# Second layer of a four-layer network: how recurrence work is dealt out over expert tiles and returning rows

## The chip, the cores and the metric

The kernel runs on one core of one Trainium2 chip, as one launch. The metric is the device time of an execution in microseconds, the median over several runs. The engines are named as in the profile: PE is TensorE, with PEld its weight loads; DVE is VectorE; ACT is ScalarE; POOL is GpSimd; SP is SyncE, which issues most DMAs.

## What is computed

Four layers follow each other; each normalises x, runs a token mixer (giving s) and a gate network (giving g), and adds s times silu(g) to x. There are 4096 tokens of 128 features: 8 sequences ("batches" in the code) of 512. The change lies in layer 1 (the second one), whose mixer is a recurrence over time and whose gate network is a mixture of experts. Cut to what matters:

```
# mixer, per sequence; r = sigmoid(mixed(xn) @ Wr); k, v = mixed(xn) @ Wk, Wv
def step(carry, kv):
    num, den, mx = carry
    max_out = maximum(mx, k + tf)
    e1, e2 = exp(mx - max_out), exp(k + tf - max_out)
    out = (e1 * num + e2 * v) / (e1 * den + e2)
    max_st = maximum(mx + td, k)
    e1s, e2s = exp(mx + td - max_st), exp(k - max_st)
    return (e1s * num + e2s * v, e1s * den + e2s, max_st), out
s = (r * out) @ Wo
# gate network: 8 routed experts, 2 per token, and 2 shared ones
g = sum_over_chosen(weight * ffn_e(xn)) + sum_over_shared(ffn_e(xn))
x = x + s * silu(g)
```

## The kernel before

Activations stay in SBUF with features on the partitions, 512 tokens (one sequence) to a block. In layer 1 `l1_layer` makes the programs of several engines go together by Python generators. All its instructions are issued through wrappers that keep the order of the code on each engine (`in_order`, so the profile gives line 82 for all of them; they are told apart by their tiles). Each engine executes its own instructions in order and waits for others by semaphores.

**The recurrence.** `attend(b)` (line 507) does one sequence in 13 parts, ended by `yield`: k; v (two products each on TensorE, copied by ScalarE); a scan for the running maximum `mx`; e1s and e2s; `mo` and e1; e2 and one Exp over all four (ScalarE, 128x2048); `ev` and the scan `num`; the scan `den` and `up`; two operations on `v` and `up`; two on `dn`; the reciprocal of `dn` (128x512); two products on `up`; and the output product `ps_o` on TensorE with its copy into s. Below, "parts" are these, and the digit before a name is the sequence. `attention(batches)` runs sequences one after the other.

**The tiles.** `experts.tiles` (line 777) works on 72 tiles of 128 gathered token rows, two in each of 36 steps, plus two steps to drain. Step t has: gathers on POOL five steps ahead (`xr`), register loads of the next expert numbers on TensorE (`which`, which may be moved earlier, as they are not held in order), the first products `ps_ab` into the two PSUM banks of `p_a`, Silu (`sa`, ScalarE) and the product `hh` (VectorE), transposes `tp_h` of the step before, second products `ps_y` of the step before that, their copy `yy` (VectorE) and its write into `yrows` by SP, and transposes `tp_g` of rows for t+2. At the end of each step parts are drawn from `between`:

```
                while done < n_between * (t + 1) // (T + 2):
                    next(between, None)
                    done += 1
```

Before, 60 parts (12 x 5) are drawn so, of the 65 of sequences 0 to 4; `for _ in between: pass` then issues the remaining five by themselves.

**The returning rows.** `experts.rows_back` (line 877) does, for each sequence b, the shared experts in four pieces (`first`: products `pa`, `pb`, Silu `a`, product `h` on VectorE; `second`: product into `acc`), then `back`: eight products that add the gathered expert rows `yr` to `acc`, and `gated`: Silu `sg`, `pr`, x. The gathers of `yr` read `yrows`, 8 per sequence, two sequences ahead (16 buffers). `first` is issued one piece ahead of `second`. After each `second` two parts are drawn, as long as b is under 5; these are sequences 5 to 7. `gated(b)` reads s of sequence b.

After this layer come the normalisation of layer 2 and the other layers, which the change does not touch.

## Time and profile before

| | |
|---|---|
| median of 5 runs | 2903.58 us (2897.37 to 2912.3) |
| profiled execution | 2910.07 us, its span 2908.4 us |
| busy: PE, DVE, ACT, POOL | 2604.9, 2195.1, 1858.4, 1552.4 us |
| first `ps_ab` of the tiles, last `ps_y` | 555.38, 739.86 us |
| first and last `acc<-ident,yr` (`back`) | 775.98, 898.69 us |
| busy in 549 to 738 us: PE, DVE, ACT | 153.74, 105.19, 85.36 us |
| busy in 738 to 757 us: PE, DVE, ACT | 4.05, 16.12, 4.75 us |
| busy in 776 to 901 us: PE, DVE, ACT | 102.51, 68.84, 36.93 us |

A row of the timeline gives start, duration, engine, line, operation, tile written and tiles read, number of instructions merged, and in brackets the idle time of that engine before it and what ended that. A group of instructions gives busy time and, behind the comma, the mean duration of one in ns; behind the bar stands the idle time of the engine just before them. A waits row gives who waited for whom: total us, times, longest.

### The profile page before, as it was taken

The page shows a single profiled execution, that of the slowest core. Times are in us where ns is not written, and L with a number is a line of the kernel's source. Part 1 is how long each engine was busy: PE and PEld are TensorE (multiplying, and loading weights), DVE is VectorE, ACT ScalarE, POOL GpSimd, SP SyncE. Part 2 cuts the span into 40 slices and gives each one's busy share as a digit, 9 for nine tenths or more (in the row PEclk, how much of TensorE's full clock was granted, in tenths as well). Part 3 has the DMA queues.
Part 4 walks back from the last instruction along what each step waited for, and adds up shares of the span by engine and source line. Part 5 has one row for each costly group of instructions (what it writes and reads, how often), then busy time and mean ns, then how long its engine had stood idle before and what let it go on. Part 6 is the DMA issues. An engine that isn't in the chain of part 4 may idle for free. (4 is left out here: it accounts for less than half of the span.)

```text
span 2908.4 us, 48757 instructions
## 1 busy us (share of the span) xinstructions
PE 2604.9 (90%) x18636; PEld 1821.2 (63%) x18636; DVE 2195.1 (75%) x2907; ACT 1858.4 (64%) x3601; POOL 1552.4 (53%) x1262
## 2 busy tenths in 40 slices
PE   7999898778778788886899999999999999999897
PEld 4656676455335555555677777777777777767675
DVE  4666554566563655554999999999999999999565
ACT  2566443245331554544698988989898888888634
POOL 2444322442342232225667778787777778787323
PEclk7899797999898888886999999999999999999979
DMA  1000002012100000002222222222122222222100
GB/s 47 2 2 2 1 1 85 24 51 50 31 28 19 2 2 2 2 1 98 60 54 59 61 61 60 61 60 55 50 64 58 61 60 61 60 52 51 25 1 30
DMA packets 56311, 112.73 MB, mean 39 GB/s; under 512 B 10768, under 2 KB 28752, under 8 KB 55440
## 3 DMA queue, kind: packets, MB, share of 16 engines
q1 hardware_dynamic: 51584, 99.40, 13.0%
q0 software_dynamic: 4352, 8.92, 1.3%
q8 instruction: 148, 2.42, 0.4%
q10 hardware_dynamic: 144, 1.31, 0.1%
q14 instruction: 83, 0.68, 0.1%
HBM read 30.43 MB, written 12.06 MB: 15 GB/s over the span
## 5 line engine op out<-in xcount | busy, mean ns | idle before, releaser
L82 POOL TENSOR_TENSOR ek<-E,kn 128x512 f32<-128x512 f32 (+3 forms) x512 | 427.7, 869 | 62.6 <-ACT kn L82 61.6
L82 POOL TENSOR_TENSOR r<-r,rs 128x1024 f32<-128x1024 f32 x128 | 317.6, 2481 | 258.4 <-DMA rs<-r 200.0
L82 POOL TENSOR_TENSOR e<-e,mx 128x1024 f32<-128x1024 f32 x112 | 212.8, 1900 | 375.2 <-DVE mx L82 287.2
L82 ACT ACTIVATE y<-y,mx 128x256 f32<-128x256 f32 (+3 forms) x512 | 287.1, 562 | 102.8 <-DVE mx L82 102.8
L82 PE MATMUL sc<-r 128*128 128x512 f32 (+3 forms) x1024 | 308.0, 444 | 24.9 <-POOL r L82 19.0
L82 PEld LDWEIGHTS ps_av<-u,at 128*128 128x128 f32 x2560 | 301.8, 192 | 41.0 <-ACT at L82 31.5
L82 PE MATMUL ps_av<-u,at 128*128 128x128 f32 x2560 | 314.7, 278 | 6.2 <-ACT at L82 6.2
L82 PEld LDWEIGHTS sc<-r 128*128 128x128 f32 x1024 | 166.2, 192 | 177.3 <-issue 70.4
L82 DVE SCALAR_TENSOR_TENSOR y<-sc,qn,V 128x512 f32<-128x512 f32 (+3 forms) x512 | 246.0, 543 | 2.3
L82 ACT ACT_TABLE_LOAD x181 | 232.2, 1283 | 4.3 <-PE pa L82 1.2
L82 DVE TENSOR_REDUCE mx<-y 128x2 f32<-128x768 f32 (+3 forms) x256 | 207.7, 812 | 1.7
L82 DVE SCALAR_TENSOR_TENSOR y<-y,coef,G 128x2560 f32<-128x2560 f32 x64 | 198.4, 3100 | 4.7 <-ACT y L82 2.3
L82 DVE SCALAR_TENSOR_TENSOR sc<-sc,ek 128x1280 f32<-128x1280 f32 x128 | 191.3, 1495 | 11.8 <-PE sc L82 6.2
L82 PE MATMUL tp<-ident,y 128*128 128x128 f32 x1280 | 197.9, 277 | 1.3 <-ACT y L82 0.8
L82 ACT COPY at<-tp 128x512 f32<-128x512 f32 (+1 forms) x384 | 188.5, 513 | 6.5 <-PE tp L82 6.4
L82 DVE TENSOR_TENSOR sc<-sc,E 128x1280 f32<-128x1280 f32 x128 | 191.1, 1493 | 0.0
L82 PEld LDWEIGHTS tp<-ident,y 128*128 128x128 f32 x1280 | 153.2, 146 | 41.7 <-issue 18.3
L82 POOL TENSOR_TENSOR s<-s,o 128x512 f32<-128x512 f32 x120 | 157.7, 1314 | 29.6 <-ACT o L82 29.6
L82 PEld LDWEIGHTS ps_u<-wvo,xn 128*128 128x128 f32 x1024 | 128.2, 191 | 70.0 <-DVE qn L82 57.0
L82 DVE TENSOR_TENSOR r<-sn,ps_kq 128x1024 f32<-128x1024 f32 x128 | 155.0, 1211 | 7.6 <-ACT sq L82 4.1
L82 ACT ACTIVATE y<-y 128x2560 f32<-128x2560 f32 x64 | 149.7, 2340 | 15.1 <-DVE y L82 7.7
L82 ACT COPY pt<-tp 128x512 f32<-128x512 f32 x224 | 121.0, 585 | 58.8 <-PE tp L82 58.6
(396 smaller groups left out, 5847.1 us busy)
## 6 DMA issues: line engine op xcount, KB each, us to landing
rs<-r SPq DMA_DIRECT2D x256, 256.0 KB
yrows<-yy SPq DMA_DIRECT2D x36, 128.0 KB
ct<-trig SPq DMA_DIRECT2D x16, 256.0 KB
m_w<-m_w SPq DMA_DIRECT2D x1, 2560.0 KB
x<-x SPq DMA_DIRECT2D x8, 256.0 KB
xrows<-row SPq DMA_DIRECT2D x8, 256.0 KB
sn<-trig SPq DMA_DIRECT2D x32, 64.0 KB
sn<-trig SPq DMA_DIRECT2D x16, 128.0 KB
```

The lines of the kernel that those rows point to most:

```text
L82: ins = op(*args, **kwargs)
```

## The change

The reciprocal of `dn` becomes four of 128x128, each a part of its own. An empty part (a second `yield`) comes between the products on `up` and the output product. A sequence so has 17 parts instead of 13. One generator over all eight sequences feeds both loops: 80 of its 136 parts are drawn in the tiles, the stop that ran the rest of sequence 4 is gone, and the remaining 56 are drawn two at a time in sequences 0 to 6 of the returning rows.

```
@@ attend
             yield
-            dve.reciprocal(dn, dn)
-            yield
+
+            for i in range(4):
+                part = slice(i * S // 4, (i + 1) * S // 4)
+                dve.reciprocal(dn[:, part], dn[:, part])
+                yield
             dve.tensor_tensor(up, up, dn, ALU.mult)
             dve.tensor_tensor(up, up, out, ALU.mult)
+            yield
             yield
             ps = pp.tile([P, S], F32, tag="ps", name="ps_o")
@@ l1_layer
         experts.route(xn, (pe, dve, act, pool), receptance)
-        MID = 5
-        between = attention(range(MID))
-        n = 12 * MID
-        experts.tiles((pe, dve, act, pool), between, n)
-        for _ in between:
-            pass
-        experts.rows_back(x, xn, s_out, (pe, dve, act, pool), attention(range(MID, B)))
+
+        between = attention(range(B))
+        experts.tiles((pe, dve, act, pool), between, 80)
+        experts.rows_back(x, xn, s_out, (pe, dve, act, pool), between)
@@ rows_back
                     second(b, n)
-                    if b < 5:
+                    if b < 7:
                         next(between, None)
                         next(between, None)
```

## The prediction, made before the changed kernel was run

> **What bounds the kernel now.** I read the page, then the busy time by stretch, and from there only the second layer's timeline, because the change touches nothing else: in the two built programs the instruction order of every engine is the same again after that layer, so whatever it gains or loses arrives at the end unchanged. The layer's two loops run from 555 to 901 us. The first question is who stops TensorE in the second loop; the answer of the waits for 746 to 910 us (total, times, longest) says:

> ```profile
> PE ps_o L82 <- DVE up L82: 27.4, 4, 15.0
> PE acc L82 <- DVE h L82: 7.3, 4, 2.6
> ```

> The output product waits four times for `up`, once for 15.0 us. The timeline shows that longest one in place (start, duration, idle before it):

> ```profile
> 739.86 2.05 PE L82 MATMUL ps_y<-m_w,hT 128*128 x16
> ...
> 743.60 0.42 DVE L82 COPY yy<-ps_y 128x256 f32<-128x256 f32 x1
> ...
> 746.92 1.45 POOL L82 DMA_INDIRECT yr<-yrows,place  x1 [43.54 <-DVE ev L82]
> ...
> 752.00 3.35 DVE L82 RECIPROCAL dn<-dn 128x512 f32<-128x512 f32 x1
> ...
> 756.86 2.08 PE L82 MATMUL ps_o<-up,a_w 128*128 128x512 f32 x2 [14.95 <-DVE up L82]
> ...
> 758.73 1.91 PE L82 MATMUL pa<-xn,m_w 128*128 128x512 f32 x2
> ...
> 775.98 1.95 PE L82 MATMUL acc<-ident,yr 128*128 128x128 f32 x16
> ```

> TensorE ends the tiles at 741.9 and stands until `for _ in between: pass` has run recurrence 4 alone on VectorE; its next products then take 1.9 us where later ones of the same form take 1.02. The windows view gives the granted clock of these stretches, the number before the DMA share:

> ```profile
> 738.00:757.00 19.00, 4.05 (x34) 3.74 (x32) 16.12 (x21) 4.75 (x5) 8.15 (x7) 0.69 0.14 41
> 757.00:776.00 19.00, 19.00 (x39) 8.26 (x40) 7.07 (x10) 6.71 (x9) 8.52 (x9) 0.86 0.12 35
> 776.00:901.00 125.00, 102.51 (x315) 51.42 (x313) 68.84 (x88) 36.93 (x51) 51.17 (x57) 0.95 0.10 28
> ```

> So an idle TensorE pays twice. Gathers of `yr` start 3.3 us after the last `yy`, and the first `back` runs at 775.98. TensorE's own timeline for the rest:

> ```profile
> 786.22 2.07 PE L82 MATMUL acc<-h,m_w 128*128 128x512 f32 x2 [2.64 <-DVE h L82]
> ...
> 794.28 1.10 PE L82 MATMUL ps_o<-up,a_w 128*128 128x512 f32 x2 [2.67 <-DVE up L82]
> ...
> 825.95 2.08 PE L82 MATMUL ps_o<-up,a_w 128*128 128x512 f32 x2 [6.07 <-DVE up L82]
> ...
> 898.69 1.95 PE L82 MATMUL acc<-ident,yr 128*128 128x128 f32 x16
> ```

> Read the brackets: each `ps_o` follows its `up` too closely. I measure everything from X, the first `hh` of the last tile pair (737.85). Before, the first `back` is at X+38.1 and the last (898.69) at X+160.8. The three batches without recurrences repeat every 12.1 us (`pr` at 866.50, 878.59, 890.68); that is TensorE's own need per batch.

> **Quarters.** The groups by form price them:

> ```profile
> L82 DVE RECIPROCAL dn<-dn 128x512 f32<-128x512 f32 x8 | 26.8, 3349 | 0.1
> L1692 DVE RECIPROCAL nrm<-nrm 128x256 f32<-128x256 f32 x1 | 1.7, 1747 | 0.0
> ```

> (3349-1747)/256 is 6.26 ns a column and leaves 145 ns per instruction, so a quarter takes 946 ns, four 3.78 us: 0.44 us more per recurrence, 3.5 us over eight, on VectorE. The bounds are 0 (the starts of independent neighbours overlap by about 0.08) and 3.5. I take 0.87 us from start to start. This is hidden wherever TensorE sets the pace, which is so for all quarter steps below. [...]

> **First loop: 80 parts instead of 60.** A bare step takes TensorE 3.27 us (`ps_ab` at 640.36 and 643.62); k or v adds 1.72, `ps_o` 0.86. VectorE needs 1.2 for two `hh` and `yy`, plus the parts. The next `ps_ab` needs the `hh` of the step before (two PSUM banks, both used), so a step costs about the larger of the two, with 1.1 us of slack. A whole reciprocal makes its step 1.2+1.4+3.35, 6.0 us; two quarters make 3.0, under 3.27. But parts now come nearly two a step everywhere: num/den/up steps 5.05, v/dn steps 4.0, and from step 27 on e2+num then den+v+dn.

> Two covers matter. After e2, VectorE idles for Exp, two table loads and Silu (3.67 us before the `hh` at 586.61). That hides under TensorE's register loads of expert numbers, which have no rows but show as gaps: 6.69 us for seven loads, 4.13 and 4.04 for five. The built order keeps 25 such loads inside the loop: groups of 7, 4, 5, 1, 3, 5 become 7, 1, 7, 1, 9, and the large groups still stand one step after the Exps of recurrences 0 to 2. Uncovered, these three would cost 3 x 3.7 = 11.

> From `ps_ab` of step 2 (566.07) to X, TensorE's own work is 126.6 (33 steps of 3.27, eight k or v, four `ps_o`, and 1.5 to `hh`); the profile has 171.8, so 45.2 of stalls: 7.6 an early stall that no row explains (569.5 to 574.7) with its slow step, the rest load gaps, slow steps behind them and reciprocals. Stepping the new order with the same durations gives: 7.6 again; 6.7, 6.7 and 8.2 for the groups, each with 2.3 of slow step; 0.8 twice for single loads; 5.7 in steps 27 to 30; 1.7 at the end; one slow step of 1.7 after the 2.7 gap there. Sum 46.8. So this loop gains nothing: X is **1.6 us later** (bounds -6 and +9, the early stall gone or doubled).

> **The seam.** The stop goes; what is late next? The last tiles now share VectorE with e2, Exp, num, den and v of recurrence 4, so the last `yy` starts at X+10.1 instead of X+5.75, and its row writes hold three things: the gathers (X+13.4 after X+9.1), and, in the built order's waits, the table load before the first shared-expert Silu, which stands in ScalarE's queue ahead of everything else there. Writes landed at X+13.4, table 1.28, Silu to X+15.2, `h` at 15.9. TensorE has done two pa/pb pairs by X+10 and stands 6 us; then (slow for 3.4 us, 1.7 lost) the three second products, two more pa/pb, ps_o, k, pa/pb, v follow without a wait, and `back` starts at **X+30.5**. Eight gathers took 11.2 us to issue (746.92 to 758.16), so X+24.6; with the 2.9 us between the end of the last `yy` and the gather that waited for its write, X+27.5. So 7.6 us earlier than before, but only three parts of recurrence 5 are done, where before it was eight.

> **Second loop.** Parts now lie in seven batches, two after each step. Per batch TensorE needs 12.1 plus k, v, ps_o: 12.1, 16.4, 12.1, 14.7, 13.8, 13.0, 12.1: 94.2. VectorE has 2.4 for `h`, 1.4 for `pr` and x, and parts; its longest batches are the first (14.9 and 2 of Exp wait), third (15.4 and 3.7) and fifth (15.9). Stepping through, with `ps_o` one step behind `up`: waits of TensorE for `h` of 2.5, 1.3, 3.6 and 2.8, for `up` of 1.2 and 1.2, one slow phase of 2.6. As an example the 3.6, in the third batch: `h` ends at X+72.2, mo and e2 (0.75 each) at 74.4 with their subtraction, Exp (1.91), table load (1.28) and Silu (0.6) reach 78.3, the next `h` 78.9; TensorE has done all it may by 75.3. Sum 15.2; the last `back` starts at X+30.5+94.2+15.2, **X+139.9**. Three of those gaps are near the 2.64 that went slow above and the 2.67 that did not: 0 to 5 us, I take 1. Against X+160.8 that is 19.9 gained; less 1.6 for X: **18 us**. Before, the same stretch cost 122.7 against a need of 94.2, 28.5 of stalls; the change halves them.

> On slow phases the rows come first: a 2.64 us gap doubled the next products, a 2.67 us one did not. [...]

> **Sum.** 2908.4 - 18 = 2890.4 of span, with the 1.7 around it 2892. The profiled execution (2910.07) is 6.5 above the median of the runs, so I take the same 18 from 2903.58: 2885.6.

> **Rivals.** *TensorE alone sets the second loop* (10%): if VectorE's lag is absorbed by the three `h` buffers, the 15.2 and the 1 go, 34 us gained, 2869. For it: 12.1 us rows without a wait; against: `acc` already waits for `h` four times, 7.3. *The gather replaces the stop* (11%): nothing shows when a gather lands; `back` at 775.98 only bounds it at 17.8 after the eighth was issued (758.2). Then `back` starts at X+42.4, 12 us later: 6 gained, 2897.6, no change. Against: row writes land in 2.9. *The first loop pays for the parts* (7%): if the load groups no longer cover the Exp waits, five waits of 3.7 stand open, with 2.3 of slow step at each: 30, less 18, **+12: 2915.6, slower**. It decides once TensorE's waits for `hh`, now 8.1 in that loop, grow by more than 18. For it: parts are denser by a third; against: the groups still stand behind three of the Exps.

> **How the numbers follow.** My forecast has 72%; its own range is 9 to 26 gained (slow phases 0 to 5, load groups +-2, the early stall other by half): 2877.5 to 2894.5. The 80% range takes in part of both neighbours: 2873 to 2898. A measurement of this kernel tells about 0.3%, 8.7 us. Faster than that: the forecast, the first rival and little of the gather: 0.83; within: 0.11; slower: 0.06.

> **What would show it.** Right: no `ps_o` wait over 3 us; the first `back` near X+30 with a TensorE gap of some 6 us before the first `acc`; quarters near 0.95; last `back` near X+140; X within 3 us of 737.85. Wrong: `back` waiting for a DMA; `hh` waits far above 8; X after 745; or an early stall of another length, which would say nothing of the edit.

## The result, and the profile after

| | before | after |
|---|---|---|
| median | 2903.83 us (65 runs, 2892.74 to 2917.48) | 2893.77 us (39 runs, 2880.66 to 2905.1) |
| profiled execution, span | 2910.07, 2908.4 us | 2894.08, 2892.4 us |

The ratio is 0.9968, 95% interval 0.9959 to 0.9977: about 9 us faster (6.7 to 12), where 18 were forecast. The two profiled spans differ by 16.0, but 5.8 of that lies ahead of the tiles: the first `ps_ab` starts at 549.62 after and at 555.38 before, and nothing there was changed. So I compare only the stretch from that `ps_ab` to the first product of the next layer (`ps` of line 129): 345.9 us before, 334.7 after, 11.2 less.

That stretch falls into three parts: the tiles (first `ps_ab` to the end of the last `hh`), the seam (from there to the first `back`) and the rows (first `back` to last). The last 2.6 us, up to the next layer, are the same in all kernels. All times in the table are read from the timelines of one execution each.

| kernel | tiles | seam | rows | all |
|---|---|---|---|---|
| before | 183.8 | 36.8 | 122.7 | 345.9 |
| after | 185.2 | 26.4 | 120.5 | 334.7 |
| after, second and third profile | 186.2, 185.2 | 26.4, 26.4 | 120.9, 120.9 | 336.1, 335.0 |
| dealing only | 188.2 | 30.5 | 125.2 | 346.6 |
| quarters only | 175.0 | 37.4 | 115.1 | 330.0 |
| after without the later part | 188.3 | 27.9 | 119.0 | 337.8 |
| after, gathers later in the program | 185.4 | 28.1 | 118.5 | 334.6 |
| after, loads apart | 170.3 | 28.1 | 119.2 | 320.3 |
| after, both edits | 172.7 | 26.4 | 120.9 | 322.6 |
| loads apart, eight buffers | 163.0 | 28.1 | 105.6 | 299.3 |
| loads apart, sg apart | 164.8 | 25.3 | 105.6 | 298.3 |
| loads apart, fewer ahead | 164.7 | 26.4 | 105.9 | 299.6 |
| all four edits | 165.6 | 25.3 | 106.0 | 299.5 |

The first five steps of the tiles hold a stall that differs between executions (see the section on the hardware): they take 35.1 us before, 37.2, 38.4 and 37.2 in the three profiles after, 38.6 with dealing only and 34.3 with quarters only. Differences of a few us between tiles can lie there.

The gain is in the seam; the rows, from which the forecast took most, give 2 us. The waits of the changed kernel from 742 to 900 us (total, times, longest):

```profile
PE acc L82 <- DVE h L82: 25.4, 7, 13.1
PE ps_o L82 <- DVE up L82: 0.8, 1, 0.8
```

`ps_o` hardly waits for `up` any more, where it waited 27.4. But `acc` waits for `h` 25.4 in the place of 7.3, and half of that is one wait. The timeline of the changed kernel shows where (start, duration, engine; in brackets the idle time before):

```profile
742.99 0.42 DVE L82 COPY yy<-ps_y 128x256 f32<-128x256 f32 x1
745.52 1.28 ACT L82 ACT_TABLE_LOAD   x1 [7.32 <-DVE dn L82]
746.31 0.94 POOL L82 DMA_INDIRECT yr<-yrows,place  x1 [46.96 <-issue]
748.19 1.12 PE L82 MATMUL acc<-h,m_w 128*128 128x512 f32 x2 [3.64 <-DVE h L82]
...
761.17 1.95 PE L82 MATMUL acc<-ident,yr 128*128 128x128 f32 x16
...
766.39 1.02 PE L82 MATMUL pb<-xn,m_w 128*128 128x512 f32 x2
776.16 0.60 ACT L82 ACTIVATE sg<-acc 128x512 f32<-128x512 f32 x1 [14.20 <-remote]
780.48 2.07 PE L82 MATMUL acc<-h,m_w 128*128 128x512 f32 x2 [13.07 <-DVE h L82]
...
881.72 1.95 PE L82 MATMUL acc<-ident,yr 128*128 128x128 f32 x16
```

Read it downward. The last `yy`, the table load and the gathers come in the order forecast, each about a microsecond sooner. The first `back` stands at 761.17. TensorE's rows then say that it had finished `back` by 763 and the next products by 767.4. Yet ScalarE starts `sg`, which needs only `back`, at 776.16; "remote" means that the profile saw nothing release it. In ScalarE's rows the Silu for the next `a` stands behind `sg` and starts at 777.62; `h` follows at 779.74 and `acc` at 780.48: TensorE is idle for 13.07 us. The windows view (PE busy first; the granted clock is the number before the DMA share) fits that: the clock, which does not come from the rows, falls from 1.00 to 0.59 where the rows show TensorE idle:

```profile
734.00:748.00 14.00, 8.01 (x28) 4.26 (x28) 10.97 (x18) 5.73 (x6) 1.38 (x2) 0.88 0.10 30
748.00:768.00 20.00, 19.22 (x56) 9.30 (x56) 6.90 (x10) 3.55 (x6) 15.13 (x16) 1.00 0.18 51
768.00:781.00 13.00, 0.52 (x1) 0.50 (x2) 2.65 (x4) 1.79 (x3) 7.08 (x7) 0.59 0.14 40
```

A reciprocal of a quarter has its own group (busy, mean ns), against 3349 ns for a whole one:

```profile
L82 DVE RECIPROCAL dn<-dn 128x128 f32<-128x128 f32 x16 | 14.0, 920 | 0.0
```

### The profile page after: what moved, and what is told of

It is laid out like the page before. It is cut to its first block, busy times and chain, and to the rows that moved or that the text cites. A ratio compares the mean times of both kernels' runs of the same rounds, so it can differ in the third digit from the quotient of the medians.

```text
span 2892.4 us, 48782 instructions
## 1 busy us (share of the span) xinstructions
PE 2596.6 (90%) x18636; PEld 1817.2 (63%) x18636; DVE 2193.7 (76%) x2931; ACT 1857.5 (64%) x3601; POOL 1548.6 (54%) x1262
## 5 line engine op out<-in xcount | busy, mean ns | idle before, releaser
L82 POOL TENSOR_TENSOR ek<-E,kn 128x512 f32<-128x512 f32 (+3 forms) x512 | 427.1, 868 | 63.2 <-ACT kn L82 62.2
L82 POOL TENSOR_TENSOR r<-r,rs 128x1024 f32<-128x1024 f32 x128 | 318.3, 2487 | 255.1 <-DMA rs<-r 224.4
L82 POOL TENSOR_TENSOR e<-e,mx 128x1024 f32<-128x1024 f32 x112 | 212.6, 1898 | 371.0 <-DVE mx L82 286.3
L82 ACT ACTIVATE y<-y,mx 128x256 f32<-128x256 f32 (+3 forms) x512 | 287.2, 562 | 102.0 <-DVE mx L82 101.8
L82 PE MATMUL sc<-r 128*128 128x512 f32 (+3 forms) x1024 | 307.9, 444 | 24.7 <-POOL r L82 18.9
L82 PEld LDWEIGHTS ps_av<-u,at 128*128 128x128 f32 x2560 | 301.8, 192 | 40.9 <-ACT at L82 31.1
L82 PE MATMUL ps_av<-u,at 128*128 128x128 f32 x2560 | 314.6, 278 | 6.2 <-ACT at L82 6.2
L82 PEld LDWEIGHTS sc<-r 128*128 128x128 f32 x1024 | 166.3, 192 | 176.6 <-issue 71.5
L82 DVE SCALAR_TENSOR_TENSOR y<-sc,qn,V 128x512 f32<-128x512 f32 (+3 forms) x512 | 246.0, 543 | 2.3
L82 DVE TENSOR_REDUCE mx<-y 128x2 f32<-128x768 f32 (+3 forms) x256 | 207.7, 812 | 1.7
L82 DVE SCALAR_TENSOR_TENSOR sc<-sc,ek 128x1280 f32<-128x1280 f32 x128 | 191.3, 1495 | 12.2 <-PE sc L82 6.2
L82 DVE SCALAR_TENSOR_TENSOR y<-y,coef,G 128x2560 f32<-128x2560 f32 x64 | 196.9, 3076 | 4.6 <-ACT y L82 2.3
L82 PE MATMUL tp<-ident,y 128*128 128x128 f32 x1280 | 197.9, 277 | 1.3 <-ACT y L82 0.8
L82 ACT COPY at<-tp 128x512 f32<-128x512 f32 (+1 forms) x384 | 188.2, 512 | 6.6 <-PE tp L82 6.5
L82 DVE TENSOR_TENSOR sc<-sc,E 128x1280 f32<-128x1280 f32 x128 | 191.2, 1493 | 0.0
L82 PEld LDWEIGHTS tp<-ident,y 128*128 128x128 f32 x1280 | 153.4, 146 | 41.7 <-issue 18.3
L82 POOL TENSOR_TENSOR s<-s,o 128x512 f32<-128x512 f32 x120 | 160.2, 1336 | 29.6 <-ACT o L82 29.6
L82 PEld LDWEIGHTS ps_u<-wvo,xn 128*128 128x128 f32 x1024 | 128.3, 191 | 69.8 <-DVE qn L82 56.0
L82 DVE TENSOR_TENSOR r<-sn,ps_kq 128x1024 f32<-128x1024 f32 x128 | 155.0, 1211 | 7.6 <-ACT sq L82 4.1
L82 ACT ACTIVATE y<-y 128x2560 f32<-128x2560 f32 x64 | 149.7, 2339 | 15.6 <-DVE y L82 7.9
L82 ACT COPY pt<-tp 128x512 f32<-128x512 f32 x224 | 120.7, 584 | 58.0 <-PE tp L82 57.8
```

The costliest lines, as they stand in the source:

```text
L82: ins = op(*args, **kwargs)
```

## The experiments

Two theories stood after the result. Either the change does what the forecast says and one stall, which may or may not belong to it, takes half the gain; or its three parts do not work as the forecast said. So the changed kernel was profiled again, beside its parts alone. Each ratio is to the kernel before on the same chip; the first seven runs were on one chip, the next three on a second and the last two on a third.

**The changed kernel again.** No edit.

> The changed kernel once more, nothing altered, for a second profile. In the first profile TensorE stands 13.07 us before an acc late in the seam (780.48), which is 10.6 us more than the forecast had there, and the whole second loop is 11.1 us longer than forecast. Theory A (the stall belongs to the change): the same acc, the third second product after the first back, again waits 8 to 15 us, the last back is again 118 to 123 us after the first. Theory B (the stall is an accident of that one execution): no wait for h over 4 us in the second loop, the last back is 107 to 113 us after the first, and the profile's span is some 10 us shorter or has a stall of this size elsewhere. Time: both 0.9968 of the kernel before, 2894 where before is 2904.

Measured: 2893.89, ratio 0.9968 (0.9951 to 0.9986). The timeline of this second profile:

```profile
776.24 0.60 ACT L82 ACTIVATE sg<-acc 128x512 f32<-128x512 f32 x1 [15.48 <-remote]
778.94 2.08 PE L82 MATMUL acc<-h,m_w 128*128 128x512 f32 x2 [12.72 <-DVE x L82]
```

The same `sg`, the same `acc`, 12.72 us; the rows take 120.9. The stall is not an accident of one execution.

**Dealing only.**

```
             dve.reciprocal(dn, dn)        # whole, as before
             ...
+        between = attention(range(B))
+        experts.tiles((pe, dve, act, pool), between, 60)
+        experts.rows_back(x, xn, s_out, (pe, dve, act, pool), between)
```

> Only the dealing out: the eight recurrences run on without a stop (60 parts in the tiles, 44 in the returning rows), but the reciprocal is whole again and the output product follows its up by one part, as before. Theory A, the seam and the even spread carry the gain: 7 to 11 us faster than the kernel before (2893 to 2897 where before is 2904), with ps_o waiting for up two or three times for 2 to 3 us in the second loop. Theory B, without quarters and the later product the dense second loop gives it back: a reciprocal of 3.35 beside 8 us of other VectorE work in a batch stops TensorE for 2.5 to 6 us in three or four batches, and the kernel is within 4 us of the kernel before.

Measured: 2900.25, ratio 1.0 (0.9982 to 1.0018). Theory B. The seam is 6.3 us shorter, but the tiles are 4.4 and the rows 2.5 longer. Of the 4.4, 3.5 lie in the first five steps. The waits of this kernel, in the tiles, and in the seam and the rows:

```profile
PE ps_ab L82 <- DVE hh L82: 16.3, 7, 7.1
...
PE ps_o L82 <- DVE up L82: 16.9, 4, 6.1
```

The first were 8.1 before, but the one of 7.1 is the stall of the first steps, which the view of the kernel before put down to "issue"; the others sum to 9.2. What the kernel gives back is in the rows: the whole reciprocals now stand in a denser stretch and still stop `ps_o` for up to 6.1.

**Quarters only.**

```
-            dve.reciprocal(dn, dn)
-            yield
+            for i in range(4):
+                part = slice(i * S // 4, (i + 1) * S // 4)
+                dve.reciprocal(dn[:, part], dn[:, part])
+                yield
...
-        n = 12 * MID
+        n = 15 * MID
...
-                    if b < 5:
+                    if b < 6:
```

> Only the quarters: the kernel before with its stop, each reciprocal in four parts (75 parts drawn in the tiles, 5 left for the stop, six batches with parts in the returning rows). By the forecast's steps the quarters are hidden and cost or bring nothing: within 3 us of the kernel before; groups of 0.95 us in the place of 3.35. Rival: they take the 3.35 us steps out of the first loop (TensorE's waits for hh, 8.1 us in the profile of before, go to 4 or less) and it is 3 to 6 us faster.

Measured: 2888.66, ratio 0.9944 (0.9926 to 0.9963). Both expectations fall short: the smallest part of the change, for which the forecast booked only a cost, is worth 15 us (11 to 21), more than the whole change. The tiles lose 8.8 us and the rows 7.6. In the kernel before, a whole reciprocal was running in eight of TensorE's waits in the tiles and the rows, 19.9 us together; here a quarter was running in two, 2.6 us together. Two of the eight in the kernel before, each behind its reciprocal:

```profile
720.26 3.35 DVE L82 RECIPROCAL dn<-dn 128x512 f32<-128x512 f32 x1
723.98 1.29 PE L82 MATMUL ps_ab<-m_w,xg 128*128 x2 [2.04 <-DVE hh L82]
...
819.34 3.35 DVE L82 RECIPROCAL dn<-dn 128x512 f32<-128x512 f32 x1
825.95 2.08 PE L82 MATMUL ps_o<-up,a_w 128*128 128x512 f32 x2 [6.07 <-DVE up L82]
```

The edit does more than shorten an instruction, though. It draws 75 parts in the tiles in the place of 60 and spreads the rest over six batches in the place of five, and the gaps that stand behind groups of register loads (below) sum to 11.6 here and to 14.9 before. So some 3 of the 15 us may belong to the loads, and what the finer dealing gives by itself was not tried.

Yet with the same quarters the changed kernel's tiles take 185. What differs stands in the gaps ahead of `ps_ab`; quarters only first, then the changed kernel:

```profile
580.88 3.78 PE L82 MATMUL ps_ab<-m_w,xg 128*128 x4 [4.22 <-DVE yy L82]
618.29 3.77 PE L82 MATMUL ps_ab<-m_w,xg 128*128 x4 [3.68 <-DVE yy L82]
655.81 3.78 PE L82 MATMUL ps_ab<-m_w,xg 128*128 x4 [3.73 <-DVE yy L82]
```

```profile
581.06 3.78 PE L82 MATMUL ps_ab<-m_w,xg 128*128 x4 [5.98 <-DVE num L82]
621.03 3.78 PE L82 MATMUL ps_ab<-m_w,xg 128*128 x4 [6.46 <-DVE num L82]
663.95 3.78 PE L82 MATMUL ps_ab<-m_w,xg 128*128 x4 [8.93 <-DVE up L82]
```

TensorE's register loads of expert numbers stand there: five in each of the first gaps, and 7, 7 and 9 in the second. The views list none of them, but the traces hold them as instructions of TensorE's sequencer: one takes 0.54 us, and in a group the next starts 1.2 us after it. The first seven of the changed kernel run from 572.12 to 580.89, and their `ps_ab` starts at 581.06; the first five with quarters only run from 574.54 to 580.72, and theirs starts at 580.88. The named releasers (`yy`, `num`, `up`) had long been done. The gaps sum to 11.6 and 21.4: that 9.7 is nearly all of the 10.2 between the two kernels' tiles.

**Without the later part.**

```
             dve.tensor_tensor(up, up, out, ALU.mult)
-            yield
             yield
...
-        experts.tiles((pe, dve, act, pool), between, 80)
+        experts.tiles((pe, dve, act, pool), between, 76)
```

> The changed kernel without the empty part ahead of the output product (16 parts each, 76 in the tiles). By the forecast the part takes the waits of ps_o for up down to 1.2 us twice; without it ps_o follows its up by one part, and waits of 1 to 2.7 us come back at five or six of eight: 4 to 9 us slower than the changed kernel, 2898 to 2903 where it is 2894. Rival: ps_o then stands behind other work anyway, and the two are within 2 us.

Measured: 2894.74, ratio 0.9971 (0.9953 to 0.999): the same as the changed kernel. The waits of the seam and the rows:

```profile
PE acc L82 <- DVE h L82: 16.0, 7, 3.8
PE ps_o L82 <- DVE up L82: 5.7, 3, 2.3
```

`ps_o` waits again, 5.7 where it was 0.8, but the 13 us wait is gone (longest 3.8): the first `sg` follows its `back` by 5.2 us here and by 15.0 in the changed kernel. So the equal times hide two opposite things. From the second `back` to the last this kernel takes 98.5 us and the changed one 91.8: the empty part is worth some 6.7 us there, inside the 4 to 9 that the forecast's steps gave.

**Gathers later, and loads apart.** The first edit moves `gather(b + 1)` behind `back(b)`. The second holds each load behind the products of its step, two steps ahead of its use:

```
             gather(0)
-            gather(1)
             first(0, 0)
...
-                if b + 2 < B:
-                    gather(b + 2)
+                if b + 1 < B:
+                    gather(b + 1)
```

```
-                if t + 1 < T:
-                    which(t + 1)
                 if t < T:
                     into(t)
+                if t + 2 < T:
+                    with tc.issue_after(mm[t].ins):
+                        which(t + 2)
```

> The changed kernel with the gathers one batch later: only gather(0) ahead of the returning rows, gather(b + 1) after back(b) in the place of gather(b + 2). In two profiles of the changed kernel TensorE's completions in the first back are recorded up to 13 us after its matmuls, while GpSimd issues sixteen gathers and then eight more without a pause; acc then waits 13.07 and 12.72 us. Theory A (the pauseless gathers make TensorE's completions late): with at most eight in a row the late stretch of the seam and the 13 us wait go, and the kernel is 6 to 11 us faster than the changed one (2883 to 2888 where that is 2894), less up to 3 us if a gather(b + 1), some 12 us from first issue to last landing, comes late for its back. Theory B (the lateness belongs to the place, the first back reading the first landed rows): the wait at the third acc after the first back stays above 8 us and the time is within 3 us of the changed kernel or slower.

> The changed kernel with TensorE's loads of expert numbers one to a step, each two steps ahead of its tiles and held behind the step's matmuls, in the place of groups of 7, 7 and 9. Theory A, groups cost and single loads do not (steps with a single load take 3.37 us against 3.27 without, a group of seven makes its step 10): the steps of 10.4, 10.3, 9.9 and 12.4 us fall to 4 to 6, the first loop from the first ps_ab to the last from 181 to 163 to 170 us, and the kernel is 9 to 16 us faster than the changed one. Theory B, the forecast's third rival in small, the groups cover VectorE's wait for Exp, two table loads and Silu: that wait of 3.7 us, with 2.3 us of slow step each, then stands open at three to five places, the first loop stays within 176 to 184 us and the kernel within 4 us of the changed one.

> Both edits in one, loads apart and gathers a batch later. If the two stalls are separate, their gains add: by Theory A of both 15 to 26 us faster than the changed kernel (2868 to 2879 where that is 2894); by Theory B of both no change; if one alone is right, the gain of that one, within 3 us.

Measured: 2887.76, ratio 0.9957 (0.9939 to 0.9976); 2877.74, 0.9912 (0.9888 to 0.9935); 2877.91, 0.9914 (0.9891 to 0.9937).

The first did not test what it was made for. The second eight gathers had free buffers, so GpSimd went on into them without a pause as before, and the wait stood again. The time lies in the range of Theory A all the same, but its interval overlaps that of the changed kernel, and the whole stretch takes what it took there (334.6 against 334.7):

```profile
776.37 2.07 PE L82 MATMUL acc<-h,m_w 128*128 128x512 f32 x2 [11.05 <-DVE x L82]
```

The second is Theory A: 16 us faster than the changed kernel, and the tiles fall from 185.2 to 170.3. With single loads nothing hides VectorE's waits for Exp, and they do stand open, as the waits in the tiles and the longest one in the timeline show:

```profile
PE ps_ab L82 <- DVE hh L82: 14.4, 8, 4.5
...
653.32 2.95 PE L82 MATMUL ps_ab<-m_w,xg 128*128 x4 [4.50 <-DVE hh L82]
```

TensorE's waits for `hh` grow from 4.4 to 14.4, but the groups cost 21.4. The group of nine made a step of 12.4 us; here that step is 7.9. The third run adds nothing to the second, as its first edit moved nothing.

**Three tries at the 13 us stall**, all on top of the loads apart: eight `yr` buffers, so that later gathers must wait for `back`; `sg` and `pr` in memory that no gather wrote, which takes eight of nine semaphores off the first `sg` and the first `pr`; and fewer tile gathers ahead.

```
-            p16 = st.enter_context(tc.tile_pool(name="f1_b16", bufs=16))
+            p16 = st.enter_context(tc.tile_pool(name="f1_b16", bufs=8))   # and gather(b + 1) behind back(b)
```

```
+        experts.p_sg = st.enter_context(tc.tile_pool(name="f1_b2", bufs=2))   # ahead of tiles
...
-            p2 = st.enter_context(tc.tile_pool(name="f1_b2", bufs=2))
+            p2 = self.p_sg
```

```
-            p12 = st.enter_context(tc.tile_pool(name="f1_12", bufs=12))
+            p12 = st.enter_context(tc.tile_pool(name="f1_12", bufs=8))
...
-            GAHEAD = 5
+            GAHEAD = 3
```

> The kernel with the loads apart, and eight yr buffers in the place of sixteen, each batch's gathers issued behind the back of the batch before. Moving gather(1) in the program alone did not shorten the run of gathers, since its buffers were free: GpSimd still issued 24 in a row and acc still waited 11.05. With eight buffers the second eight can start only when the first back has read the first. Theory A (the run of gathers makes TensorE's completions late): the 12 us wait after the first back falls to 4 or less, the kernel is 6 to 11 us faster than with the loads apart alone (2867 to 2872 where that is 2878), less what later gathers cost at the following backs, at most 2 us each as a batch of 13 us or more covers 12. Theory B (it belongs to the place): acc again waits 8 to 13 us there.

> The kernel with the loads apart, and the buffers of sg and pr opened ahead of the tiles, so that they lie in no memory that gathers wrote; the first sg and the first pr then wait for one semaphore each in the place of nine, and GpSimd's gathers stay as they are. Theory C (the eight added waits on the gathers' semaphores, taken by ScalarE and VectorE just then, hold TensorE's signals or the two engines): the 12 us wait goes and the kernel is 6 to 11 us faster than with the loads apart alone. Theories A and B: the wait stays above 8 us and the time within 3 us of that kernel.

> The kernel with the loads apart, and the tiles' gathers three steps ahead with eight xr buffers in the place of five and twelve. The same lateness of TensorE's completions stands at the first steps of the tiles in every profile so far (it ends 15 to 23 us after the first ps_ab), with a stall of 5 to 8 us and a step of 8 to 14 us. Theory A: with eight gathers in a row at the start in the place of twelve the early stall falls by half or goes, 3 to 6 us faster than with the loads apart alone. Theory B: the stall stays at 5 to 8 us; if gathers three steps ahead come late, tp_g waits for xr and it is slower by 2 to 10.

Measured: 2864.34, ratio 0.9892 (0.9865 to 0.9919); 2856.28, 0.9861 (0.9836 to 0.9886); 2857.66, 0.9868 (0.9843 to 0.9894). The stall is gone in all three: rows 105.6, 105.6 and 105.9. The third leaves the seam alone and the first two leave the tiles alone, but the tiles too are 5.5 to 7.3 us shorter in each than with the loads apart alone. Each edit removed what it could not touch, so these three do not tell the theories apart: they ran on another chip.

**The changed kernel and all edits together, on one chip.**

> The changed kernel a third time, because in the last three runs, all on another chip than the ones before, TensorE's completions were on time everywhere, also at the early place that two of the three edits do not touch. Theory D (the lateness belongs to the chip and the execution, not to the kernel): where it is absent the stall of 13 us and the early one are absent in the changed kernel as well, its second loop takes 105 to 107 us from first back to last in the place of 120.6, its layer some 20 us less, and its ratio to the kernel before falls to 0.990 to 0.994; where the lateness is present the ratio stays at 0.9968 and the loop at 120 to 121. Theory E (the three edits removed it): the stall of 12 to 13 us stands here again whatever the chip, ratio 0.9968.

> Loads apart, eight yr buffers, sg and pr in memory of their own, three steps ahead with eight xr buffers: all edits in one kernel. Theory D: on a chip where the changed kernel shows late completions this one shows them too, 2870 to 2880; where it does not, 2852 to 2862. Theory E: no late completions and 2852 to 2862 on any chip.

Measured: 2891.13, ratio 0.9957 (0.9938 to 0.9976); 2862.64, 0.9856 (0.9827 to 0.9886). The timeline around the first `back`, of the changed kernel and then of the other:

```profile
758.13 1.95 PE L82 MATMUL acc<-ident,yr 128*128 128x128 f32 x16
...
773.03 0.60 ACT L82 ACTIVATE sg<-acc 128x512 f32<-128x512 f32 x1 [14.11 <-remote]
778.08 2.07 PE L82 MATMUL acc<-h,m_w 128*128 128x512 f32 x2 [13.71 <-DVE h L82]
```

```profile
737.73 1.95 PE L82 MATMUL acc<-ident,yr 128*128 128x128 f32 x16
739.71 0.60 ACT L82 ACTIVATE sg<-acc 128x512 f32<-128x512 f32 x1 [1.20 <-PE acc L82]
```

On the same chip, in one profile of each, `sg` follows its `back` by 14.9 us in one kernel and by 2.0 in the other. So the stall at the seam goes with the kernel, against Theory D. The lateness at the first steps of the tiles is another matter: it stands in every profile on the first and third chip, in this last kernel as well, and in none of the three on the second. Which of the four edits frees the seam was not separated, and whether the changed kernel would stall on the second chip was not tried. The last kernel and the one with `sg` apart are the fastest here, about 1.4% below the kernel before.

## Why the prediction was right, and where it was wrong

Sign and range held; the size did not, and the inside of the sum was off at three places that partly cancel. That the time lies in the range is in part luck: no step of the forecast held the stall of some 10 us at the seam.

- **Tiles.** Forecast 1.6 us later (measured to X, the first `hh` of the last pair). X lies 182.5 us after the first `ps_ab` before and 184.3, 185.4 and 184.3 in the three profiles after: 1.8 to 2.9. All of it lies in the first five steps (35.1 before; 37.2, 38.4 and 37.2 after), where the stall that differs between executions stands, so the agreement says little of the edit. The groups of loads, forecast 6.7, 6.7 and 8.2, were 5.98, 6.46 and 8.93. The single loads, forecast 0.8 each, cost 0.1 (steps of 3.37 against 3.27).
- **But "gains nothing" was a balance of two large terms.** Quarters alone take 8.8 us out of the tiles; the larger load groups of the changed program put it back (9.7 of gaps). The forecast saw the groups as a cover that would cost 11 if it went. The loads apart show the reverse: they cost 21.4 to hide 10.
- **Quarters.** The price was right, 920 ns where 946 was worked out. The step that failed is "hidden": it counted what four instructions add and not which stalls a 3.35 us block on VectorE had been causing outside the stop. Here four quarters take 0.33 us more than a whole (four of 920 ns against 3349), and quarters alone make the kernel 15 us faster: what whole reciprocals block (19.9 us of waits beside them, 2.6 beside quarters) outweighed the 0.33, though the finer dealing came with the edit and was not tried apart.
- **Seam.** Forecast first `back` at X+30.5, measured X+27.2 in all three profiles. The chain was as described; `yy` came at X+9.1 and the gathers at X+12.4, a microsecond early each, the gap ahead of `acc` was 3.64 in the place of 6, and no slow phase followed it. The second rival, gathers late for `back`, is out: `back` waited for none. The profile before could have said so: the trace holds the updates of the gathers' semaphores, and those on record for the eighth end at 759.67, 1.5 us after its issue had ended at 758.15.
- **Rows.** Forecast 109.4 us from first `back` to last, measured 120.5 to 120.9. Of the waits for `h` forecast as 2.5, 1.3, 3.6 and 2.8, the first was 13.07; the others were 1.33, 3.04 and 2.13, with two small ones of 1.54 and 0.63 besides. Waits for `up`, forecast twice 1.2, were once 0.8. So one term is mis-sized, by 10.6, which is about what the rows lack. No step of the forecast held a late `sg`. Where it is absent the rows take 105.6 to 106.0, 3.5 us better than forecast; with such rows the changed layer would be some 26 us shorter than before, not 18 (an estimate: those rows were measured in kernels with further edits).
- **Rivals.** TensorE alone as the bound did not happen: without the stall `acc` still waits 7.6 in the rows. The first loop paying for the parts did not happen in the changed kernel (`hh` waits 4.4, not above 26), and where the cover was taken away on purpose those waits grew by 10.

As a whole: the change is quarters (15 us gained alone), dealing (nothing alone) and the later part (some 7 in the rows). Together they give 10, because in combination they bring the larger load groups and the stall. Dealing only keeps nearly the groups of the kernel before (single loads left out, 6, 4, 5, 3 and 5 against 7, 4, 5, 3 and 5), and quarters only has 5, 5, 5 and 3; dealing with quarters makes them 7, 7 and 7, and with the later part 7, 7 and 9. None of the kernels that lack a part has the whole stall: there `sg` follows the first `back` by 2.9 to 5.2 us, against 14.9 to 16.3 in the three profiles of the changed kernel. Put on top of the quarters, dealing and later part shorten the seam by 11.0 us, lengthen the tiles by 10.2 and the rows by 5.5.

## What to carry to other kernels

Price each part of a change for what it takes away as well as for what it adds, also where its place seems covered; then run the parts alone, since here the smallest edit beat the whole. Instructions that the views do not list, such as register loads, are worth looking up in the trace or in the built order wherever a gap names a releaser that was long done: spread one to a step they cost 0.1 us each, in groups of seven to nine some 0.9. When an engine waits for "remote" long after the named producer's row has ended, go by the consumer's start and not by the end of that row: in the changed kernel the row of the first `back` ends at 763.12, and `sg` started at 776.16, 0.03 us after the last increment on record.

## What the runs showed of the hardware that was not expected

**Completions that come late.** In the changed kernel's trace seven increments of TensorE's semaphore are on record for the eight products of the first `back`: at 762.62, 765.49, 767.61, 771.14, 773.95, 776.09 and 776.13, the first six 2 to 3.5 us apart; at the second `back` they come 0.22 apart. ScalarE's `sg` starts 0.03 us after the last of them, and the gathers of GpSimd that need these buffers 0.26 us after theirs. TensorE's rows and the granted clock (1.00 up to 768, 0.59 from there to 781) suggest that the products themselves were done by 767.4. The gathers were not late: the last one for the first `back` had landed by 757.8. What holds the increments is open. A long run of gathers was under way each time, but in the kernel before sixteen gathers ran from 746.9 to 768.2 beside TensorE's products without it.

The place of the first `back` among the gathers goes with the stall in all profiles but those of the second chip. Where the sixteenth gather had ended on GpSimd ahead of the first `back` (by 7.8 us in the kernel before, 5.5 with quarters only, 1.6 with dealing only), `sg` followed that `back` by 3.9, 3.9 and 2.9 us. Where it ended 1.9 behind (without the later part), `sg` followed by 5.2, and where it ended 4.0 to 5.3 behind (the changed kernel, gathers later in the program, loads apart, both), by 12.6 to 16.3. With eight buffers, in the last kernel, only eight gathers came ahead of the first `back`, and `sg` followed by 2.0. An earlier first `back` is what the change was made for, so the stall may be its price. But on the second chip `sg` followed by 2.0 even where the sixteenth gather ended 5.4 and 6.7 behind (fewer ahead, `sg` apart), so this is not shown. Nor is it shown that the recording has no part in it: of the 16 semaphore records of a gather, 3 to 8 are there for the third to the eighth in the changed kernel, and all 16 for every gather in the three profiles of the second chip, where no increment is late.

**The same gap, at full clock once and at half clock once.** The same `acc`, after the same idle time, in the changed kernel and in the one with fewer gathers ahead:

```profile
822.72 1.12 PE L82 MATMUL acc<-h,m_w 128*128 128x512 f32 x2 [3.04 <-DVE h L82]
```

```profile
782.06 2.08 PE L82 MATMUL acc<-h,m_w 128*128 128x512 f32 x2 [3.04 <-DVE h L82]
```

A gap of 3.04 us cost nothing in one, and in the other the next products took twice as long; in the changed kernel 1.12 us followed a gap of 3.64 and 2.01 us one of 2.13.

```profile
818.14:821.55 3.41, 1.54 (x4) 1.00 0.15 38
821.55:824.97 3.42, 2.25 (x14) 1.00 0.00 0
...
859.10:862.51 3.41, 1.28 (x4) 1.00 0.14 38
862.51:865.93 3.42, 3.42 (x4) 0.50 0.19 58
```

```profile
778.40:781.81 3.41, 0.62 (x2) 1.00 0.08 19
781.81:785.22 3.41, 3.16 (x9) 0.50 0.01 2
```

From the first `ps_ab` to the last `back` of all fourteen traces, the clock halved behind every one of 100 full-clock windows with more than 1.97 us idle and behind none of 1008 with less than 1.95; of ten between, eight halved. From half it came back only behind windows with less than 0.6 us idle. The forecast's pair of gaps in the kernel before differs in the same way: 2.64 us in one window, 2.67 as 1.46 and 1.21 in two. So the length of a gap alone does not tell what it costs here.
